# A two-layer graph kernel: h_prime turned by DMA, edge masks made on GpSimd, and layer 0 stretched over 42 steps

## The chip, the cores and the metric

The kernel runs on one core of one Trainium2 chip. The metric is the device time of one execution in microseconds (us), as the median of three runs. A core has five engines that run side by side and wait for each other with semaphores: TensorE (PE in the profile, with PEld for its weight loads), VectorE (DVE), ScalarE (ACT), GpSimd (POOL) and SyncE (SP), which here only issues DMAs. Sixteen DMA engines move data between the chip's main memory (HBM) and the on-chip memory (SBUF). TensorE writes its results to another on-chip memory, PSUM.

## The reference

There are 16 batches of 1024 nodes with 128 features each, and an adjacency matrix of zeros and ones per batch. Two layers follow each other. Everything is float32. Cut to what matters:

```python
# layer 0, B, N, D = 16, 1024, 128
h = einsum('bnf,df->bnd', x, Ww) + Wb
e = einsum('bjl,bkl->bjk', einsum('bjd,dl->bjl', h, A), h)
e = e + swapaxes(e, 1, 2)                       # symmetric scores
scores = where(adj > 0, e, 0.0)
attention = softmax(scores, axis=1) * adj
h_prime = relu(einsum('bij,bjk->bik', attention, h))
ic = sigmoid(h_prime @ wi_u + x @ wi_x)[..., None]
fc = sigmoid(h_prime @ wf_u + x @ wf_x)[..., None]
oc = sigmoid(h_prime @ wo_u + x @ wo_x)[..., None]
x = layernorm(x + oc * tanh(ic * h_prime + fc * x))

# layer 1, H = 4 heads
h = einsum('bnf,hfd->hbnd', X, conv_w) + conv_b[:, None, None, :]
scores = einsum('hbni,hij,hbmj->hbnm', h, attn_w, h)
Ah = tanh(A[None] * scores)
hh = relu(einsum('hbnm,hbmd->hbnd', Ah, h))
x = layernorm(x + relu(relu(mean(hh, axis=0)) + X))
```

## The kernel before

The rows of a batch are worked on in eight blocks of 128. The main loop runs layer 1 of batch b, in 32 steps (4 heads by 8 blocks), and puts pieces of layer 0 of batch b+1 between the steps. One step of layer 1:

```python
def layer1_step(b, hd, m):
    ...
    for q in range(NH):                                   # two halves of 512 columns
        ps = ps_sc.tile([P, 512], F32, tag="sc", ...)     # four PSUM banks turn by turn
        nc.tensor.matmul(ps, x1T[:, ts(m, P)], uT[:, ts(q, 512)], start=True, stop=True)
        nc.vector.tensor_mul(s[:, ts(q, 512)], ps, adj[:, ts(q, 512)])
    nc.scalar.activation(s, s, AF.Tanh)
    def back(halves=range(NH)):
        for q in halves:
            nc.tensor.matmul(acc[:, ts(q, 512)], h1[:, ts(hd, D)], s[:, ts(q, 512)], ...)
    ...
    push(...)          # back is issued two steps later
```

A float32 matmul shows in the profile as two records, called passes below. A step is thus eight passes of 512 columns.

The pieces of layer 0 have letters: L loads xT and the eight adjacency tiles of a batch, X loads x, Q and H project, S makes a block of scores (upper triangle), T turns it into the lower triangle, A masks and exponentiates a block, B multiplies it by the adjacency and feeds the matmul of the block before, R is the relu, P and p bring h_prime from columns to rows, G makes the gates, and I, O, V, N make the output and its layernorm.

```python
def mask(j):                                              # A
    s = t["R"][:, :, j, :]
    if ("edge", j) in t:                                  # batch 0
        ... nc.vector.tensor_tensor_reduce(s[:, ks], s[:, ks], t["edge", j][:, ks], 1.0, top, ALU.mult, ALU.max, highest)
        nc.vector.tensor_scalar_mul(nmax, highest, -1.0)
    else:                                                 # all other batches
        nc.vector.scalar_tensor_tensor(s, adj, 0.0, s, op0=ALU.is_gt, op1=ALU.mult)
        nc.vector.tensor_reduce(nmax, s, AX.XY, ALU.max, negate=True)
    nc.scalar.activation(s, s, AF.Exp, bias=nmax, accum_out=t["z", j])

def weigh(j):                                             # B
    nc.vector.tensor_mul(s, s, adj_t[b][j]...)            # line 353
    nc.vector.reciprocal(rz, t["z", j])
    nc.scalar.mul(t["hz", j], t["h"][:, j, :D], rz)
    if j:
        back(j - 1)                                       # four passes of 512 columns

def rows_hp(groups):                                      # P, p: h_prime to rows, by TensorE
    for ks in groups:
        for i, k in enumerate(ks):                        # ident_g: identity and the three w*_u columns
            nc.tensor.matmul(pt[:, i, :], t["hpT"][:, ts(k, P)], ident_g, start=True, stop=True)
        nc.scalar.copy(t["hp"][:, ks[0] : ks[-1] + 1, :], pt)
```

In batch 0 the edges (adjacency above zero, as bf16) are made by GpSimd in `find_edges`, one `tensor_scalar` per block. Other turns go without TensorE: VectorE transposes within 32x32 squares, one DMA writes the result to HBM, and four DMAs read it back in the other order.

```python
def turn(dst, src, name):
    t = sb.tile([P, N], F32, tag="turn", bufs=2, ...)
    nc.vector.transpose(t..., src)
    nc.sync.dma_start(d, t)
    for c in range(P // Q):                               # 4
        nc.sync.dma_start(dst[ts(c, Q)]..., dv[c])
```

The plan of the steps, and the loop:

```python
BETWEEN = [
    "H0 H1 H2", "S0", "T0 S1", "T1 S2", "T2 A0", "S3 B0", "T3 A1", "S4 B1",
    "T4 A2", "S5 B2", "T5 A3", "S6 B3", "T6 A4", "S7 B4", "A5", "B5",
    "A6", "B6", "A7", "B7", "X R", "P", "p G", "I0",
    "O0", "V0", "N0", "", "", "", "", "",
]
AHEAD = {28: "L", 31: "Q0 Q1"}                            # for batch b+2
TURN = 27                                                 # x1 of batch b+1 is turned
ENDING = (DELAY, DELAY + 3, DELAY + 5, DELAY + 7)         # end of layer 1 of batch b-1
for b in range(B):
    after = layer0(b + 2) if b + 2 < B else {}
    for step in range(H * NB):
        hd, m = divmod(step, NB)
        layer1_step(b, hd, m)
        ...                                               # rows(b, second half) in step 0
        run(nxt, BETWEEN[step])
        if step == TURN and b + 1 < B: turn_x1(b + 1)
        run(after, AHEAD.get(step, ""))
        ...                                               # head_uT once a head, rows(b+1, first half) in step 31
```

Ahead of the loop stands a start in which layer 0 of batch 0 runs alone and that of batch 1 begins.

Of the kernel before, what the change touches and what calls it, by code (L numbers as in the profile page):

```python
# [11 lines left out]
F32 = mybir.dt.float32  # L12
BF16 = mybir.dt.bfloat16
AF = mybir.ActivationFunctionType
# [4 lines left out]
P = 128  # L19
# [4 lines left out]
def two_layer_adjacency_kernel(  # L24
# [44 lines left out]
    a_in = consts.tile([P, P], F32, name="a_in")  # L69
    nc.sync.dma_start(a_in, A)  # L70
    ww_in = consts.tile([P, P], F32, name="ww_in")
# [19 lines left out]

    def load_late_weights():
        nc.sync.dma_start(cw_in[0:1], conv_b.rearrange("(o h) d -> o h d", o=1))
        nc.sync.dma_start(cw_in[1:P], conv_w[:, 0 : D - 1, :].rearrange("h f d -> f h d"))
        nc.sync.dma_start(cw_last, conv_w[:, D - 1 : D, :].rearrange("h f d -> f h d"))
        nc.sync.dma_start(aw, attn_w.rearrange("h i j -> i h j"))

# [6 lines left out]
    but_first = consts.tile([1, P], F32, name="but_first")  # L104
# [10 lines left out]
    a_sym = consts.tile([P, P], F32, name="a_sym")  # L115
    s_ww = consts.tile([P, P], F32, name="s_ww")
# [3 lines left out]
    b_wide = consts.tile([P, P], F32, name="b_wide")  # L120
# [116 lines left out]
    def layer0(b):  # L237
# [7 lines left out]
        def load():  # L245
            t["xT"] = sb.tile([P, N], F32, tag="xT", name=f"xT_{b}")
            nc.sync.dma_start(t["xT"], xT[b])
            adj_t[b] = []
            for j in range(NB):
                a = adjp.tile([P, N], F32, tag="adj", name=f"adj_{b}_{j}")  # L250
                nc.sync.dma_start(a, adjT[b, ts(j, P), :])
                adj_t[b].append(a)
# [72 lines left out]
        def find_edges(j):  # L325

            m = sb.tile([P, N], BF16, tag="h1", name=f"edge_{b}_{j}", bufs=NB + 1)
            nc.gpsimd.tensor_scalar(m, adj_t[b][j], 0.0, None, ALU.is_gt)
            t["edge", j] = m.rearrange("p (k d) -> p k d", d=P)

        def mask(j):
            s = t["R"][:, :, j, :]
            nmax = sb.tile([P, 1], F32, tag="nmax", name=f"nmax_{b}_{j}", bufs=4)
            if ("edge", j) in t:
                top = -3e38
                for q, ks in enumerate((ts(0, BH), ts(1, BH)) if j == 0 else [slice(NB)]):
                    highest = sb.tile([P, 1], F32, tag="highest", name=f"highest_{b}_{j}_{q}", bufs=4)
                    nc.vector.tensor_tensor_reduce(
                        s[:, ks], s[:, ks], t["edge", j][:, ks], 1.0, top, ALU.mult, ALU.max, highest
                    )  # L340
                    top = highest
                nc.vector.tensor_scalar_mul(nmax, highest, -1.0)
            else:
                adj = adj_t[b][j].rearrange("p (k d) -> p k d", d=P)
                nc.vector.scalar_tensor_tensor(s, adj, 0.0, s, op0=ALU.is_gt, op1=ALU.mult)  # L345
                nc.vector.tensor_reduce(nmax, s, AX.XY, ALU.max, negate=True)  # L346
            t["z", j] = sb.tile([P, 1], F32, tag="z", name=f"z_{b}_{j}", bufs=4)
            nc.scalar.activation(s, s, AF.Exp, bias=nmax, accum_out=t["z", j])  # L348

        def weigh(j):  # L350

            s = t["R"][:, :, j, :]
            nc.vector.tensor_mul(s, s, adj_t[b][j].rearrange("p (k d) -> p k d", d=P))  # L353
            rz = sb.tile([P, 1], F32, tag="rz", name=f"rz_{b}_{j}", bufs=4)
            nc.vector.reciprocal(rz, t["z", j])  # L355
            t["hz", j] = sb.tile([P, D], F32, tag="hz", name=f"hz_{b}_{j}", bufs=4)
            nc.scalar.mul(t["hz", j], t["h"][:, j, :D], rz)  # L357
            if j:
                back(j - 1)
# [27 lines left out]
        def gates():  # L387

            gate = t["gate"]
            gflat = gate.rearrange("p k g -> p (k g)")  # L390
            nc.vector.tensor_add(gate, t["hp"][:, :, D : D + 3], gate)
            nc.scalar.activation(gflat, gflat, AF.Exp, scale=-1.0)
            nc.vector.tensor_scalar_add(gflat, gflat, 1.0)
            nc.vector.reciprocal(gflat, gflat)  # L394
            t["u"] = sb.tile([P, NB, D], F32, tag="u", name=f"u0_{b}", bufs=1)
            t["x1"] = sb.tile([P, NB, D + 1], F32, tag="x1", name=f"x1_{b}")
            for ks in PARTS:
                nc.gpsimd.tensor_mul(  # L398
                    t["u"][:, ks], t["x"][:, ks],
                    gate[:, ks, 1:2].to_broadcast([P, ks.stop - ks.start, D]),  # L400
                )
            nc.gpsimd.memset(t["x1"][:, :, 0:1], 1.0)

# [21 lines left out]
        def finish(p):  # L425
# [7 lines left out]
            "L": load, "X": load_x, "R": relu,  # L433
            "P": lambda: rows_hp(GROUPS[:-1]), "p": lambda: rows_hp(GROUPS[-1:]),
            "G": gates,
        }
        for i, ks in enumerate(GROUPS):
            pieces[f"H{i}"] = partial(project_h, [ks])
# [7 lines left out]
        for j in range(NB):  # L446
            for name, piece in (("S", score), ("A", mask), ("B", weigh)):
                pieces[f"{name}{j}"] = partial(piece, j)
            if b == 0:
                pieces[f"E{j}"] = partial(find_edges, j)  # L450
            if j + 1 < NB:
                pieces[f"T{j}"] = partial(turn_score, j)
# [40 lines left out]
    def layer1_step(b, hd, m):  # L493
        x1T, h1, uT = x1T_t[b], h1_t[b, m], u_t[b, hd]
        adj = adj_t[b][m]
# [62 lines left out]
    def last_end(b, k0, k1):  # L558
# [19 lines left out]
    run(first, "L X")  # L578
    load_late_weights()
    run(second, "L")  # L580
# [8 lines left out]
    run(first, "P p G")  # L589
# [14 lines left out]
    run(second, "T0 T1 T2")  # L604
# [4 lines left out]
    BETWEEN = [  # L609
        "H0 H1 H2", "S0", "T0 S1", "T1 S2", "T2 A0", "S3 B0", "T3 A1", "S4 B1",  # L610
        "T4 A2", "S5 B2", "T5 A3", "S6 B3", "T6 A4", "S7 B4", "A5", "B5",
        "A6", "B6", "A7", "B7", "X R", "P", "p G", "I0",
        "O0", "V0", "N0", "", "", "", "", "",
    ]
    AHEAD = {28: "L", 31: "Q0 Q1"}
    TURN = 27
    ENDING = (DELAY, DELAY + 3, DELAY + 5, DELAY + 7)
    end, nxt = None, second
    for b in range(B):
        after = layer0(b + 2) if b + 2 < B else {}  # L620
        for step in range(H * NB):
            hd, m = divmod(step, NB)
            layer1_step(b, hd, m)
            if b and step == 0:
                rows(b, range(NB // 2, NB))
            if end is not None and step in ENDING:
                next(end, None)
            run(nxt, BETWEEN[step])
            if step == TURN and b + 1 < B:
                turn_x1(b + 1)  # L630
            run(after, AHEAD.get(step, ""))
            if hd == H - 1 and b + 1 < B:
                if m == NB - 1:
                    head_uT(b + 1, 0)
                    rows(b + 1, range(NB // 2))
            elif hd < H - 1 and m == NB - 4:
                head_uT(b, hd + 1)
# [55 lines left out]
```

## Time and profile before

| What | Value |
|---|---|
| time, median of three runs | 2448.36 us (2446.39 to 2449.8) |
| span of the profiled execution | 2444.8 us |
| granted TensorE clock, mean | 0.999 of full |
| mean DMA rate | 74 GB/s |
| DMA packets | 409,057, of which 352,630 are under 512 B |

"Busy" is the time in which an engine has at least one instruction under way. A line of the groups gives source line, engine, operation, operands and count, then busy time and the mean duration of one. The costliest groups on VectorE, ScalarE and GpSimd that the change touches are these.

| Line | Engine | What | Count | Mean ns |
|---|---|---|---|---|
| L345 | DVE | mask, batches 1 to 15 | 120 | 1195 |
| L346 | DVE | maximum, batches 1 to 15 | 120 | 1220 |
| L338 | DVE | fused mask and maximum, batch 0, whole blocks | 7 | 1210 |
| L353 | DVE | weighing by adjacency | 128 | 1240 |
| L328 | POOL | edges, batch 0 | 8 | 2950 |
| L384 | PE | h_prime to rows, passes of 131 columns | 256 | 275 |
| L385 | ACT | copy of these rows, two sizes | 32 and 16 | 488 and 378 |
| L398 | POOL | x times forget gate, batches 1 to 15 | 15 | 1900 |
| L556 | POOL | issue of an output store | 15 | 970 |

Durations of matmuls overlap, since the next begins before the last has drained. How long a matmul holds TensorE is read from the starts.

### The profile page before, as it was taken

To read this page: it belongs to the slowest core of one execution; us is meant where nothing else is said; L and a number is where in the kernel's file an instruction comes from. 1 tells how busy PE (TensorE), PEld (TensorE's weight loads), DVE (VectorE), ACT (ScalarE), POOL (GpSimd) and SP (SyncE) were. 2 spreads that over 40 slices of the span, in tenths; PEclk is the share of its full clock that TensorE was granted. 3 is DMA by queue.
4 is the path that set the end of the run, shared out by engine and by line. 5 is a ranking of instruction groups with operands and counts; after the bars stand their busy time and mean duration, and the time that the engine had idled before them with its cause. 6 is when DMAs were issued, how large, how long until landed. Compare 5 with 4: busy or idle time off the path is not lost.

```text
span 2444.8 us, 19911 instructions
## 1 busy us (share of the span) xinstructions
PE 2427.2 (99%) x6175; PEld 1121.6 (46%) x6175; DVE 1585.3 (65%) x3026; ACT 1083.9 (44%) x1522; POOL 136.5 (6%) x102
## 2 busy tenths in 40 slices
PE   8999999999999999999999999999999999999998
PEld 4444444444444444444444444444444444444444
DVE  6665847657586565866658666585765857658454
ACT  6444444344444444434444444444444444444432
POOL 4000000000000000000000000000000000000000
PEclk9999999999999999999999999999999999999999
DMA  4204124051230512304133140332404223042000
GB/s 174 60 10 145 45 95 95 1 151 39 95 95 9 148 34 101 89 21 142 27 108 81 52 124 15 119 70 72 106 12 128 62 95 84 11 135 55 17 26 9
DMA packets 409057, 180.77 MB, mean 74 GB/s; under 512 B 352630, under 2 KB 377078, under 8 KB 408951
## 3 DMA queue, kind: packets, MB, share of 16 engines
q1 hardware_dynamic: 405927, 171.63, 25.2%
q0 software_dynamic: 2160, 7.87, 0.8%
q8 instruction: 49, 0.80, 0.1%
q14 instruction: 57, 0.47, 0.1%
q10 hardware_dynamic: 864, 0.00, 0.0%
HBM read 127.80 MB, written 51.64 MB: 73 GB/s over the span
## 4 chain that ended last, share of the span: by engine, by line
PE 94%; DVE 2%; DMA 2%; SPq 1%; issue 0%; POOL 0%; ACT 0%; POOLq 0%; DVEq 0%
PE sc L510 34%; PE acc L516 34%; PE acc L365 9%; PE sc L288 5%; PE pT_u L201 4%; PE pR L481 4%; PE pT_q L201 1%; PE pt L384 1%; PE pR_h L272 1%; DMA xT<-in_xT_dram 1%; SPq L230 1%; DMA dram_x<-turn_x 0%; DVE st L184 0%; DVE x L192 0%; POOL rs L189 0%
## 5 line engine op out<-in xcount | busy, mean ns | idle before, releaser
L511 DVE TENSOR_TENSOR s<-sc,adj 128x512 f32<-128x512 f32 x1008 | 671.5, 685 | 623.0 <-PE sc L510 611.0
L510 PE MATMUL sc<-uT,x1T 128*128 128x512 f32 x2048 | 962.0, 592 | 0.0
L516 PE MATMUL acc<-s,h 128*128 128x512 f32 x2016 | 947.3, 592 | 0.0
L512 ACT ACTIVATE s<-s 128x1024 f32<-128x1024 f32 x504 | 533.0, 1057 | 806.9 <-DVE s L511 800.5
L516 PEld LDWEIGHTS acc<-s,h 128*128 128x128 f32 x2016 | 381.7, 190 | 483.5 <-issue 474.4
L510 PEld LDWEIGHTS sc<-uT,x1T 128*128 128x128 f32 x2048 | 385.7, 190 | 468.8 <-issue 421.7
L365 PE MATMUL acc<-R,hz 128*128 128x512 f32 x512 | 241.1, 593 | 1.5 <-ACT hz L357 1.4
L348 ACT ACTIVATE R<-R,nmax 128x1024 f32<-128x1024 f32 x128 | 147.0, 1149 | 201.9 <-DVE nmax L346 182.2
L353 DVE TENSOR_TENSOR R<-R,adj 128x1024 f32<-128x1024 f32 x128 | 158.7, 1240 | 5.7 <-issue 0.3
L346 DVE TENSOR_REDUCE nmax<-R 128x1 f32<-128x1024 f32 x120 | 146.4, 1220 | 4.1
L288 PE MATMUL sc<-xT,qT 128*128 128x512 f32 (+3 forms) x384 | 146.5, 491 | 0.5 <-ACT R L291 0.5
L365 PEld LDWEIGHTS acc<-R,hz 128*128 128x128 f32 x512 | 95.6, 190 | 108.0 <-issue 85.1
L345 DVE SCALAR_TENSOR_TENSOR R<-adj,R 128x1024 f32<-128x1024 f32 x120 | 143.3, 1195 | 0.0
L189 POOL TENSOR_TENSOR rs<-rs,mhalf 128x8 f32<-128x8 f32 (+2 forms) x35 | 65.8, 1881 | 1207.0 <-DVE rs L188 948.3
L291 ACT ACTIVATE R<-sc,h 128x512 f32<-128x512 f32 (+1 forms) x192 | 109.4, 579 | 39.2 <-PE sc L288 37.7
L201 PE MATMUL pT_u<-x1T,ms 128*128 128x512 f32 x256 | 120.4, 592 | 0.0
L481 PE MATMUL pR<-cw,x1T 128*128 128x512 f32 x256 | 114.9, 592 | 0.0
L357 ACT ACTIVATE hz<-h,rz 128x128 f32<-128x128 f32 x128 | 51.3, 400 | 128.7 <-DVE rz L355 128.4
L288 PEld LDWEIGHTS sc<-xT,qT 128*128 128x128 f32 x384 | 70.1, 192 | 70.4 <-issue 58.0
L484 ACT COPY h<-pR 128x512 f32<-128x512 f32 x128 | 75.0, 586 | 41.7 <-PE pR L481 41.7
L398 POOL TENSOR_TENSOR u<-x,gate 128x1024 f32<-128x1024 f32 (+1 forms) x17 | 30.6, 1799 | 969.4 <-DVE gate L394 969.4
L534 DVE SCALAR_TENSOR_TENSOR sum<-acc,sum 128x512 f32<-128x512 f32 x95 | 61.2, 686 | 33.8 <-PE acc L516 32.9
(109 smaller groups left out, 1035.2 us busy)
## 6 DMA issues: line engine op xcount, KB each, us to landing
adj<-in_adjT_dram SPq DMA_DIRECT2D x128, 512.0 KB, 7.7
xT<-in_xT_dram SPq DMA_DIRECT2D x16, 512.0 KB, 4.5
x<-in_x_dram SPq DMA_DIRECT2D x16, 512.0 KB, 4.2
dram_x<-turn_x SPq DMA_DIRECT2D x15, 512.0 KB, 2.6
x1T<-dram_x SPq DMA_DIRECT2D x60, 128.0 KB, 3.1
dram_sum<-turn_sum SPq DMA_DIRECT2D x15, 512.0 KB, 2.6
y<-dram_sum SPq DMA_DIRECT2D x60, 128.0 KB, 3.1
out_dram<-y POOLq DMA_DIRECT2D x15, 512.0 KB, 3.5
```

Source lines behind the costliest of these rows:

```text
L201: nc.tensor.matmul(ps, w, src[:, ts(q, 512)], start=True, stop=True)
L288: nc.tensor.matmul(ps[:, : at - lo], t["qT"][:, ts(j, P)], t["xT"][:, lo:at], start=True, stop=True)
L345: nc.vector.scalar_tensor_tensor(s, adj, 0.0, s, op0=ALU.is_gt, op1=ALU.mult)
L346: nc.vector.tensor_reduce(nmax, s, AX.XY, ALU.max, negate=True)
L348: nc.scalar.activation(s, s, AF.Exp, bias=nmax, accum_out=t["z", j])
L353: nc.vector.tensor_mul(s, s, adj_t[b][j].rearrange("p (k d) -> p k d", d=P))
L365: nc.tensor.matmul(t["acc"][:, ts(q, 512)], t["hz", j], t["R"][:, ts(q, BH), j, :], start=(j == 0), stop=(j == NB - 1),)
L481: nc.tensor.matmul(ps, x1T_t[b][:, ts(k, P)], cw.rearrange("p h d -> p (h d)"), start=True, stop=True)
L510: nc.tensor.matmul(ps, x1T[:, ts(m, P)], uT[:, ts(q, 512)], start=True, stop=True)
L511: nc.vector.tensor_mul(s[:, ts(q, 512)], ps, adj[:, ts(q, 512)])
L512: nc.scalar.activation(s, s, AF.Tanh)
L516: nc.tensor.matmul(acc[:, ts(q, 512)], h1[:, ts(hd, D)], s[:, ts(q, 512)], start=(m == 0), stop=(m == NB - 1),)
```

## The change

The change has four parts and a few moves of buffers.

1. In batches 1 to 15 h_prime gets to rows by a turn and a hop through HBM (`turn_hp`), not by `rows_hp` on TensorE. The products with the three gate vectors, which `ident_g` used to give along with the rows, are made by GpSimd (a multiplication with a broadcast vector) and VectorE (a sum along features). It is meant to take work from TensorE.
2. In all batches GpSimd makes the edges, as bytes in batches 1 to 15, and VectorE masks and takes the maximum in one instruction.
3. Layer 0 of a batch is spread over 42 steps: it begins in step 17 of the loop two batches earlier (`AHEAD`) and goes on to step 26 of the next one. Batch 1, which starts later, has a denser plan of its own (`FIRST`). It is meant to give the longer path of h_prime its room.
4. The adjacency tiles are loaded one by one, from GpSimd's queue from batch 2 on, each two steps ahead of its edges.

The diff, cut to its core:

```diff
-        def load():
-            t["xT"] = ...; nc.sync.dma_start(t["xT"], xT[b])
-            for j in range(NB): ... nc.sync.dma_start(a, adjT[b, ts(j, P), :])
+        def load_xT(): ...
+        def load_adj(j):
+            a = adj_t[b, j] = adjp.tile([P, N], F32, tag="adj", name=f"adj_{b}_{j}")
+            (nc.sync if b < 2 else nc.gpsimd).dma_start(a, adjT[b, ts(j, P), :])
 ...
         def find_edges(j):
-            m = sb.tile([P, N], BF16, tag="h1", ...)
+            if b == 0: m = sb.tile([P, N], BF16, tag="h1", ...)
+            else:      m = sb.tile([P, N], U8, tag="edge", ...)      # two buffers
 ...
         def mask(j):
-            (batch 0 fused, others scalar_tensor_tensor and tensor_reduce)
+            s, nmax = t["R"][:, :, j, :], -3e38
+            for ks in (ts(0, BH), ts(1, BH)) if (b, j) == (0, 0) else [slice(NB)]:
+                nc.vector.tensor_tensor_reduce(s[:, ks], s[:, ks], t["edge", j][:, ks], 1.0, nmax, ALU.mult, ALU.max, top)
 ...
+        def turn_hp():
+            t["hp"] = sb.tile([P, NB, D], F32, tag="hp", ...)
+            turn(t["hp"]..., hpT, f"hp_{b}")
+        def weigh_hp():
+            for g in (1, 0, 2):
+                t["hw", g] = sb.tile([P, NB, D], F32, tag="turn", ..., bufs=2)
+                nc.gpsimd.tensor_mul(t["hw", g], t["hp"], wu_b[:, g : g + 1, :].to_broadcast([P, NB, D]))
+        def sum_hp(g):
+            nc.vector.tensor_reduce(hw, t["hw", g], AX.X, ALU.add)
+            nc.vector.tensor_add(gate, hw, gate)
+        def gate_f():   sum_hp(1); sigmoid(t["gate"][:, :, 1:2]); forget()
+        def gate_i():   sum_hp(0)
+        def gates_io(): sum_hp(2); sigmoid(t["gate"][:, :, 0:3:2])
 ...
+        if b == 0: pieces.update(P=lambda: rows_hp(GROUPS), G=gates)
+        else:      pieces.update(P=turn_hp, Y=weigh_hp, F=gate_f, i=gate_i, o=gates_io)
 ...
+        for g, w in enumerate((wi_u, wf_u, wo_u)):        # with the late weights, at the start
+            nc.sync.dma_start(wu_b[:, g, :], w.partition_broadcast(P))
 ...
-    BETWEEN = [...]; AHEAD = {28: "L", 31: "Q0 Q1"}
+    BETWEEN = {
+        0: "L7 E5 B1 A3 T5 S6", 1: "B2", 2: "E6 A4", 3: "B3 S7 T6", 4: "E7 A5", 5: "B4", 7: "A6",
+        8: "B5", 10: "A7 B6", 11: "B7", 12: "X R", 13: "P", 16: "Y", 18: "F", 19: "i", 20: "o",
+        21: "I0", 22: "O0", 23: "V0", 26: "N0",
+    }
+    AHEAD = {
+        17: "W", 18: "Q0 Q1", 19: "H0 H1 H2", 20: "S0", 21: "T0 S1", 22: "S2", 23: "S3", 24: "T1",
+        25: "L0 T2 S4", 26: "L1", 27: "L2 E0 T3", 28: "L3 E1 S5", 29: "L4 A0 E2 T4",
+        30: "L5 A1 E3", 31: "L6 B0 A2 E4",
+    }
+    FIRST = {
+        0: "E1 A0 T3 S4", 1: "E2 B0 A1 T4 S5", 2: "E3 A2 T5 S6", 3: "E4 B1 A3 T6 S7",
+        4: "E5 B2 A4", 5: "E6 B3 A5", 6: "E7 B4 A6", 7: "B5 A7",
+    }
-    ENDING = (DELAY, DELAY + 3, DELAY + 5, DELAY + 7)
+    ENDING = (DELAY, 6, 12, 14)
+        plan = BETWEEN if b else {**BETWEEN, **FIRST}
```

Some tiles of the start that had buffers of their own (the weights `a_in`, `ww_in`, `a_sym`, `s_ww`, and `b_wide`, `but_first`) now share those of `hz` and `uT1`.

## Prediction

> **What bounds the kernel now.** I read the engine totals first. The columns are busy time, share of the span and instructions.
>
> ```profile
> span 2444.8 us, 19911 instructions
> PE 2427.2 (99%) x6175; PEld 1121.6 (46%) x6175; DVE 1585.3 (65%) x3026; ACT 1083.9 (44%) x1522; POOL 136.5 (6%) x102
> ```
>
> TensorE (PE) is busy 99% of the time and the next engine, VectorE (DVE), 65%. A busy TensorE can still be a slow one, because overlapping matmuls count as busy, so I went on to its waits (engine, line, releaser; total, times, longest).
>
> ```profile
> PE pw L122 <- DMA a_in<-in_L_gnn_A_dram: 3.2, 1, 3.2
> PE pt L565 <- DVE sum L534: 1.6, 1, 1.6
> PE pT_q L201 <- DMA xT<-in_xT_dram: 1.6, 5, 0.7
> PE acc L365 <- ACT hz L357: 1.4, 4, 0.5
> ```
>
> These are the four longest of eleven entries, and the eleven add up to 11 us. Only the third lies in the steady part of the program: TensorE reaches `pT_q` at the end of a batch slightly before the x tile has landed. The others are start and end.
>
> Then the timeline of TensorE near the end of layer 0 of one batch (start, busy time, what, how many).
>
> ```profile
> 761.40 1.88 PE L510 MATMUL sc<-uT,x1T 128*128 128x512 f32 x4
> 763.12 1.88 PE L516 MATMUL acc<-s,h 128*128 128x512 f32 x4
> 764.84 1.50 PE L384 MATMUL pt<-ident_g,hpT 128*128 128x131 f32 x12
> 766.18 1.88 PE L510 MATMUL sc<-uT,x1T 128*128 128x512 f32 x4
> 767.89 1.88 PE L516 MATMUL acc<-s,h 128*128 128x512 f32 x4
> 769.61 0.61 PE L384 MATMUL pt<-ident_g,hpT 128*128 128x131 f32 x4
> 770.06 1.88 PE L510 MATMUL sc<-uT,x1T 128*128 128x512 f32 x4
> ```
>
> Here starts matter, not durations. Four 128x512 passes occupy 763.12 - 761.40 = 1.72 us, so 0.43 us each, with or without layer 0 work between them. Twelve 128x131 passes take 766.18 - 764.84 = 1.34 us, which is 0.112 us each. Taking 381 columns off saves 0.318 us, or 0.833 ns a column, and 3 ns are left over per pass. So the pass rate is set by columns streamed and nothing waits.
>
> Last, busy time of each engine in two whole batches.
>
> ```profile
> 350.00:500.40 150.40, 150.40 (x381) 69.31 (x380) 99.34 (x188) 67.17 (x94) 7.05 (x5) 1.00 0.27 77
> 500.40:650.80 150.40, 150.40 (x381) 69.23 (x380) 99.36 (x188) 67.26 (x95) 7.05 (x5) 1.00 0.28 77
> ```
>
> After the stretch come its length, then PE, PEld, DVE, ACT and POOL, clock, DMA share and GB/s. A batch costs 150.40 us. The passes of a batch in the code give the same: 32 steps x 8 passes, 16 for `head_uT`, 16 for `rows`, 4 for `project_q` and 32 for layer 0's `back` are 324 x 0.4295 = 139.2; the scores are 9216 columns in 24 passes, 7.75; `project_h` 16 x 0.1125 = 1.8; `rows_hp` 1.79. Sum 150.5. The kernel is TensorE's own work plus a start of about 70 us and a short end.
>
> **What the Trainium skill says.** "Perfetto Trace Analysis", Identifying the Most-Contended Engine, warns that matmul busy share is no measure of distance from the limit and asks for weight-load share or useful work instead. The trace shows why (46% for weight loads beside 99%), so I rely on start-to-start times. "TensorE: Matmul & The Clock Gate", Back-to-back issue gap, has a gap that is linear in columns with about 2.5 ns on top; the trace agrees on the form and the constant (3 ns), while the column costs 0.833 ns here, twice the page's, in each of an f32 matmul's two recorded passes. "SBUF — State Buffer", Who interferes with whom, says that VectorE with two SBUF inputs and a GpSimd instruction reading SBUF lock each other out. The start of the trace agrees only in part: while GpSimd makes edges without pause, the multiplication of line 353 takes 1.85 us instead of 1.22, less than a whole 2.8 us edge, and the fused mask keeps its 1.20 us. "DMA: Bandwidth & Descriptors", SWDGE vs HWDGE vs iDMA, says that GpSimd builds the descriptors of DMAs in its queue. The 15 output stores of the kernel before show it as 0.97 us of GpSimd each.
>
> **The change, part by part.**
>
> TensorE. In batches 1 to 15 `rows_hp` goes: 8 matmuls, 16 passes x 0.112 = 1.79 us a batch, x 15 = 26.9 us. Batch 0 keeps its own. `turn_hp`, as `turn_x1` does already, needs no TensorE. Nothing is added to it. This is the whole direct gain, since the other engines' savings lie beside a TensorE that doesn't wait. The x tile for `project_q` is now asked for in step 17 rather than after the turn of x1 at step 27, with DMA traffic low, so the 1.6 us of waits should go too.
>
> VectorE, per batch. Removed: 8 x (1.195 + 1.220) = 19.3 us of mask and maximum. Added: 8 x (1.21 + 0.08 + 0.15) = 11.5 for fused mask, accumulator read and negation, with durations from batch 0 of the same trace; one turn 1.23; three reductions 3 x 1.22 = 3.7; their small additions 0.5; a second sigmoid 0.5. That is 99.3 - 19.3 + 11.5 + 1.2 + 3.7 + 0.5 + 0.5 = 97.4. If all eight multiplications of line 353 meet an edge, 8 x 0.63 = 5 more. So 97 to 102 of 148.6 us: an even exchange, and not the bound.
>
> ScalarE loses three copies (2 x 0.488 + 0.378 = 1.35) and gains one small exponential, about 0.2. No matter.
>
> GpSimd, per batch: 7.05 now, plus eight edges of 2.76 to 3.2, plus three 128x1024 multiplications of 1.9, plus eight loads of 0.97: 43 to 46 us, or 30%. Edges and loads lie in steps 25 to 4, twelve steps. These last about 12 x 3.43 for layer 1, three `uT` (5.2), `rows` (6.9) and some 10 of layer 0, together about 63 us, against 8 x (3.0 + 0.97) = 32. It keeps up, if it isn't held.
>
> Slack of the new waits, a bare step being 8 x 0.4295 = 3.43 us. (a) h_prime: relu in step 12, turn in 13. The x1 turn in the trace writes at 790.50, reads from 793.18 to 795.92, and its last read takes about 3, so landing is 8 us after the issue, 9 with VectorE. Step 18, where VectorE first needs the product, is over 17 us after step 13; less 9 and 1.9 for GpSimd, 6 us are free. (b) Adjacency: load in step 25+j, edge in 27+j, so about 7 to 9 us against an estimated 1 + 4.2 (GpSimd's 0.97, and the 4.2 in which 512 KB of x landed). (c) Edge j to mask j is two steps, and with two edge buffers edge j+2 waits for mask j: 3 us of work in a whole step or more. (d) Batch 1, over eleven steps, has the shortest paths: four turns one after another on the sync queue, some 5.7 us each, for steps of 4 to 7 us. Here a few us may be lost, once.
>
> The sum: 2448.4 - 26.9 - 1.6, plus 1.5 allowed for the start (three broadcast weight loads now stand before batch 1's x in the queue) and for (d), gives 2421.4. A quick look at density: steps 21 to 27 ask VectorE for 3.3 to 4.9 us each while TensorE has 3.4 to 4.9 there, because the next batch's scores now fall in the same steps. That is close, but in the kernel before, VectorE was full for 20 us on end (690 to 710) without a TensorE wait.
>
> **The rivals.** First, VectorE held by GpSimd: if an edge comes late, the mask stands at the head of VectorE's queue, layer 1's multiplications queue behind it and TensorE runs out of its four score banks. For it: GpSimd's queue now holds loads that wait for tiles, edges that wait for loads and for masks. Against it: the two-step distances above. One wait of 2 us in each of 15 batches would more than cancel the gain (2451); 5 us would give 2496. Second, port contention stretches VectorE by 0.63 us in many more instructions than line 353, and the dense steps tip over: perhaps 0.5 to 1 us a batch, 2430 to 2437. Third, the hop is hidden but more small packets delay the other turns: the hop adds one turn to the nine of a batch (seven of scores, x1 and the sum), so perhaps a tenth to a DMA share of 0.27, which doesn't fill it; no change. Fourth, the smoother plan gains more than the passes removed: there is nothing to gain, as steady TensorE has only 1.6 us of waits.
>
> **Range and chances.** The floor is solid: 15 x 1.79 plus all 11 us of waits would be 2410, and a 2% gain needs 2399, so 0.02 for faster by over 2%. Upward, one small wait a batch gives 2430 to 2437, hence 2416 to 2434 for eight in ten. Slower than 2497 needs over 5 us a batch lost: 0.03.
>
> **What would show it.** Right: a batch period near 148.6 us, all of it TensorE busy; no `pt` matmuls beyond batch 0's 16 passes; the fused mask at about 1.2 us x120 more; GpSimd near 30%. Wrong: TensorE waits in every batch that go back to masks or edges, VectorE waits on GpSimd of over 2 us, line 353 at 1.85 or more throughout, or a start longer than 70 us by more than 2.

## The result, and the profile after

| | before | after |
|---|---|---|
| time, median | 2447.93 us (2446.39 to 2449.80, 4 runs) | 2502.64 us (2502.54 to 2503.06, 4 runs) |
| ratio after / before | | 1.0223, 95% interval 1.0206 to 1.0241 |
| span of the profiled execution | 2444.8 us | 2500.3 us |
| granted TensorE clock, mean | 0.999 | 0.987 |

The change made the kernel 2.2% slower. The prediction was 2421.4 us, so 81.2 us have to be found. The engine totals of the changed kernel (busy time, share of the span, instructions):

```profile
span 2500.3 us, 20182 instructions
PE 2428.7 (97%) x5935; PEld 1103.2 (44%) x5935; DVE 1606.2 (64%) x3266; ACT 1074.8 (43%) x1492; POOL 629.3 (25%) x379
```

TensorE has 240 passes fewer, which is 15 x 16 as planned, and yet more busy time. VectorE (64%) and GpSimd (25%) are no fuller than foreseen. The longest waits of TensorE in the changed kernel (what waits, line, what released it; total us, times, longest):

```profile
PE pT_u L207 <- DMA x1T<-dram_x: 45.0, 12, 4.5
PE pT_u L207 <- DVE nmax L349: 8.3, 2, 4.4
PE pw L128 <- DMA a_in<-in_L_gnn_A_dram: 3.2, 1, 3.2
```

The first two are new. `pT_u` is the first product of layer 1 of the next batch, `head_uT(b+1, 0)`, and its operand `x1T` is the turned x1. It waits once in 14 batches, 53.3 us in all. The second line is the same wait, at the same place and of the same length (3.9 and 4.4 us): in these two batches the record of a VectorE instruction happens to fall within 0.03 us of TensorE's start. TensorE's timeline at one such place (start, busy time, what, how many, and in brackets the wait ahead of it):

```profile
673.58 1.88 PE L557 MATMUL acc<-s,h 128*128 128x512 f32 x4
679.02 3.37 PE L207 MATMUL pT_u<-x1T,ms 128*128 128x512 f32 x4 [3.56 <-DMA x1T<-dram_x]
682.23 3.60 PE L522 MATMUL pR<-cw,x1T 128*128 128x512 f32 x8
```

TensorE stands for 3.56 us, and then the four passes of `pT_u` occupy 682.23 - 679.02 = 3.21 us instead of 1.72. That is a second loss, and the windows of the changed kernel show what goes with it. The columns are stretch, length, PE, PEld, DVE, ACT, POOL, granted clock, DMA share and GB/s. The first stretch runs from the issue of x1's write to that of its first read, the second from there to the start of `pT_u`, and the third holds `pT_u`'s passes.

```profile
666.50:672.70 6.20, 6.20 (x15) 2.66 (x14) 2.30 (x5) 2.66 (x4) 3.32 (x2) 1.00 0.75 204
672.70:679.00 6.30, 2.76 (x7) 0.96 (x6) 6.21 (x11) 3.76 (x5) 3.25 (x2) 0.96 0.93 206
679.00:682.20 3.20, 3.18 (x4) 1.44 (x5) 0.54 (x3) 1.83 (x3) 2.79 (x2) 0.55 0.66 188
```

After the wait the granted clock is 0.55. The records of the clock in this trace have it at half for 3.41 us at ten of the 14 waits and for twice that at the other four. Over the whole run the `pT_u` passes are busy 143.8 us against 120.4 before, and the `pR` passes 119.6 against 114.9: 28.1 us more. Waits 53.3 and slow passes 28.1 make 81.4, against a distance to the prediction of 81.2.

Why x1 is late is seen in the queue of SyncE. In the kernel before (start, time to issue, what, how many):

```profile
790.50 0.34 SPq L227 DMA_DIRECT2D dram_x<-turn_x  x1
793.18 2.74 SPq L230 DMA_DIRECT2D x1T<-dram_x  x4
795.97 0.82 SPq L247 DMA_DIRECT2D xT<-in_xT_dram  x1
796.83 4.73 SPq L251 DMA_DIRECT2D adj<-in_adjT_dram  x8
```

The loads of the next batch stand behind the hop of x1 in the same queue, so the write has no load beside it: 2.7 us until the reads are issued. In the changed kernel:

```profile
657.75 0.59 SPq L323 DMA_DIRECT2D dram<-turn  x1
663.27 2.82 SPq L326 DMA_DIRECT2D R<-dram  x4
666.50 0.32 SPq L233 DMA_DIRECT2D dram_x<-turn_x  x1
672.68 3.67 SPq L236 DMA_DIRECT2D x1T<-dram_x  x4
676.45 0.75 SPq L323 DMA_DIRECT2D dram<-turn  x1
```

A turn of scores (T2, first two lines) now goes ahead of x1: VectorE began to turn x1 at 662.09, but its write comes 4.4 us after that, when T2's reads have been issued. Then it takes 6.2 us. An adjacency load went out of GpSimd's queue at 665.82, 0.7 us ahead of the write. The median times from issue to landing in the changed kernel (KB each, us) say the same of all batches:

```profile
adj<-in_adjT_dram POOLq DMA_DIRECT2D x112, 512.0 KB, 4.4
...
dram_hp<-turn_hp SPq DMA_DIRECT2D x15, 512.0 KB, 2.6
...
dram_x<-turn_x SPq DMA_DIRECT2D x15, 512.0 KB, 6.3
x1T<-dram_x SPq DMA_DIRECT2D x60, 128.0 KB, 3.7
```

The write of h_prime has the size and form of x1's and lies in steps without loads: 2.6 us. x1's takes 6.3, where in the kernel before it took

```profile
dram_x<-turn_x SPq DMA_DIRECT2D x15, 512.0 KB, 2.6
```

One thing more lies on this path. The layernorm's last piece (`x<-u,mv,rs`), which the turn follows, has grown, as VectorE's groups show (busy us, mean ns of one | idle before). Before:

```profile
L192 DVE TENSOR_SCALAR x<-u,mv,rs 128x128 f32<-128x128 f32 x128 | 34.3, 341 | 10.0 <-POOL rs L189 9.8
```

After:

```profile
L198 DVE TENSOR_SCALAR x<-u,mv,rs 128x128 f32<-128x128 f32 x128 | 66.5, 726 | 0.1
```

In the batch above, its eight instructions take 4.39 us instead of 2.14, from 656.58, while GpSimd makes an edge (2.80 us from 657.51).

So the theory: x1's hop lost its slack to three things, (i) the layernorm stretched by an edge, (ii) a turn of scores ahead of it in the sync queue, (iii) adjacency loads beside its write and reads. The rivals: GpSimd's edges hold VectorE (the prediction's first rival); the removal of one cause is enough; or the third and fourth part of the change are at fault as a whole, and nothing in it gains.

### The profile page after: what moved, and what is told of

Read it like the earlier page. It is cut to its first block, busy times and chain, and to the rows that moved or that the text cites. A ratio compares the mean times of both kernels' runs of the same rounds, so it can differ in the third digit from the quotient of the medians.

```text
span 2500.3 us, 20182 instructions
## 1 busy us (share of the span) xinstructions
PE 2428.7 (97%) x5935; PEld 1103.2 (44%) x5935; DVE 1606.2 (64%) x3266; ACT 1074.8 (43%) x1492; POOL 629.3 (25%) x379
## 4 chain that ended last, share of the span: by engine, by line
PE 88%; DMA 7%; SPq 3%; DVE 1%; issue 0%; ACT 0%; POOL 0%; POOLq 0%; DVEq 0%; ACTq 0%
PE sc L551 32%; PE acc L557 31%; PE acc L368 8%; PE pT_u L207 5%; PE pR L522 5%; PE sc L294 4%; DMA dram_x<-turn_x 3%; DMA x1T<-dram_x 2%; SPq L236 1%; DMA dram<-turn 1%; PE pT_q L207 1%; PE pR_h L278 1%; SPq L99 1%; SPq L326 1%; DVE s L552 0%
## 5 line engine op out<-in xcount | busy, mean ns | idle before, releaser
L552 DVE TENSOR_TENSOR s<-sc,adj 128x512 f32<-128x512 f32 x1008 | 680.4, 686 | 702.7 <-PE sc L551 691.2
L337 POOL TENSOR_SCALAR edge<-adj 128x1024 uint8<-128x1024 f32 (+1 forms) x128 | 356.3, 2785 | 463.3 <-DVE top_None L344 455.3
L195 POOL TENSOR_TENSOR rs<-rs,mhalf 128x8 f32<-128x8 f32 (+2 forms) x35 | 54.6, 1561 | 973.7 <-DVE rs L194 973.7
L207 PE MATMUL pT_u<-x1T,ms 128*128 128x512 f32 x256 | 143.8, 691 | 53.4 <-DMA x1T<-dram_x 45.0
L344 DVE CUSTOM_DVE_ANT_0 R<-R,edge 128x1024 f32<-128x1024 f32 (+1 forms) x128 | 154.1, 1204 | 3.5 <-PE turn L312 3.4
L399 POOL TENSOR_TENSOR hw<-hp,wu_b 128x1024 f32<-128x1024 f32 x45 | 107.1, 2396 | 145.0 <-DVE s L552 44.6
L522 PE MATMUL pR<-cw,x1T 128*128 128x512 f32 x256 | 119.6, 612 | 0.0
L319 DVE STREAM_TRANSPOSE turn<-R 128x896 f32<-128x896 f32 (+6 forms) x105 | 73.6, 701 | 62.0 <-DMA dram_x<-turn_x 54.1
L207 PEld LDWEIGHTS pT_u<-x1T,ms 128*128 128x128 f32 x256 | 53.9, 218 | 126.3 <-issue 54.3
L258 POOL DMA_DIRECT2D adj<-in_adjT_dram x112 | 65.8, 588 | 133.6 <-DVE s L552 133.4
```

The lines of the kernel that those rows point to most:

```text
L207: nc.tensor.matmul(ps, w, src[:, ts(q, 512)], start=True, stop=True)
L337: nc.gpsimd.tensor_scalar(m, adj_t[b, j], 0.0, None, ALU.is_gt)
L522: nc.tensor.matmul(ps, x1T_t[b][:, ts(k, P)], cw.rearrange("p h d -> p (h d)"), start=True, stop=True)
```

## The experiments

Every kernel is the changed one with the edit shown. Those run several times have an interval against the kernel before on the same chip. The others ran once, which suffices for differences of 20 us and more: the widest of the repeated sets (the first experiment, 8 runs) spans 15 us.

**Start x1 earlier.** The layernorm goes from step 26 to 24, the turn of x1 from 27 to 25.

```diff
-        21: "I0", 22: "O0", 23: "V0", 26: "N0",
+        21: "I0", 22: "O0", 23: "V0", 24: "N0",
-    TURN = 27
+    TURN = 25
```

> Edit: the layernorm's last piece N0 moves from step 26 to 24 and the turn of x1 from step 27 to 25, nothing else. Theory (the turn of x1 lands too late for the first projection of the next batch, and that wait is the whole loss): the turn starts two steps (7 us) earlier, the wait was 3 to 4.5 us, so the wait and the slow clock behind it go; batch period 148.6 us, time 2419 to 2427. Rival (GpSimd's edges and waits hold VectorE, and TensorE waits for that): VectorE's steps 24 and 25 become denser, so the time stays at 2500 or gets worse.

Measured: 2454.75 us (2450.93 to 2466.11, 8 runs), ratio 1.0040 (1.0024 to 1.0056). 48 us came back and the wait at `pT_u` is gone. But the time isn't near 2421, since waits have moved. From the waits of this kernel (its profiled execution took 2464.67 us, 10 more than the median, so they are on the high side):

```profile
DVE turn L319 <- DMA dram<-turn: 50.9, 17, 4.5
...
PE pR L522 <- ACT uT L209: 28.2, 14, 2.9
DVE turn L319 <- DMA dram_x<-turn_x: 24.7, 12, 5.0
```

VectorE stands 75.6 us before turning scores, because both buffers for turned tiles are held by writes that haven't landed. ScalarE's copy of `uT` then comes late, and TensorE waits for it one step behind `pT_u`. That the buffers cause it is the reading here; the three-buffer version below tests it.

**No adjacency traffic.** From batch 2 on a batch uses the tiles of the batch two before it. It leaves out 112 of the 128 adjacency loads, and all later batches are computed with the adjacencies of the first two, so only its time is of use.

```diff
         def load_adj(j):
+            if b >= 2:
+                adj_t[b, j] = adj_t[b - 2, j]
+                return
```

> Edit: the adjacency loads of batches 2 to 15 are left out; these batches use the tiles of batch b-2, so the output is of other adjacencies, and the DMA engines carry 59 MB less. Theory (the loads share the DMA engines with the turn of x1 and stretch it): the write of x1 lands in 2.6 to 3.3 us, not 6.2, the score turn before it in the queue is 2 us shorter too, together more than the wait of 3 to 4.5 us; time 2420 to 2430. If the order of the sync queue or the stretched layernorm on VectorE is enough to make the wait, 2450 to 2500.

Measured: 2423.79 us, x1's write 2.9 us in the mean. All of the loss is gone. But the edges no longer wait for loads and moved too (the layernorm is back at 2.13 us), so (i) and (iii) are taken away together. A later run separates them.

**x1 ahead of the turns of scores.**

```diff
-        25: "L0 T2 S4", 26: "L1", 27: "L2 E0 T3", 28: "L3 E1 S5", 29: "L4 A0 E2 T4",
-        30: "L5 A1 E3", 31: "L6 B0 A2 E4",
+        25: "L0 S4", 26: "L1", 27: "L2 E0", 28: "L3 E1 T2 S5", 29: "L4 A0 E2 T3",
+        30: "L5 A1 E3 T4", 31: "L6 B0 A2 E4",
```

> Edit: the score turns T2, T3, T4 of the batch after next move from steps 25, 27, 29 to 28, 29, 30, behind the turn of x1 in the sync queue. Theory (in the queue x1 stands 3 us behind the reads of T2): the write of x1 is issued about 3 us earlier, but still takes some 6 us beside the loads; wait 0.5 to 1.5 us a batch, time 2430 to 2450. If the order in the queue doesn't matter, 2500.

Measured: 2482.51 us, 20 us less than the changed kernel, and a miss. x1 is now nearly in time (0.1 us of wait a batch at `pT_u`). But the three turns have been crowded behind x1's write, which still takes 5.0 us beside loads, and VectorE waits for their buffers. TensorE loses 31.8 us at `pR` to ScalarE's copy of `uT` and 6.7 more to VectorE. The layernorm is as stretched as before (725 ns a piece). The queue's order alone is not the cure.

**No edges on GpSimd.** Batches 1 to 15 mask as the kernel before did.

```diff
         def find_edges(j):
+            if b: return
 ...
+                nc.vector.scalar_tensor_tensor(s, adj, 0.0, s, op0=ALU.is_gt, op1=ALU.mult)
+                nc.vector.tensor_reduce(nmax, s, AX.XY, ALU.max, negate=True)
```

> Edit: batches 1 to 15 make no edges on GpSimd and mask with two VectorE instructions as the kernel before did (8 us more of VectorE a batch); the loads stay on GpSimd's queue. Theory: the last piece of the layernorm takes 2.1 us again instead of 4.4, but x1 still stands behind T2 in the sync queue and beside the loads, so the wait stays within 1 us of what it was: 2490 to 2505. Rival (edges on GpSimd hold VectorE or take its port): without them the time falls to 2420 to 2430.

Measured: 2527.40 us, 25 us slower than the changed kernel and outside both ranges: late edges are not what costs the time. TensorE waits at `pT_u` for 50.1 + 19.7 us. The layernorm is short again, and x1's turn starts 2 us earlier, but its write is issued 6.3 us after the turn instead of 4.4, since T2's hop ahead of it now takes longer: the loads are no longer spaced by edges. That last step is argued from the times of issue.

**A third buffer for turned tiles.** (The tile xT moves to one buffer to make room, and that of batch 1 into one of x1T's.)

```diff
-    tag="turn", bufs=2
+    tag="turn", bufs=3                 # all tiles of this tag
-            t["xT"] = sb.tile([P, N], F32, tag="xT", ..., bufs=2)
+            t["xT"] = sb.tile([P, N], F32, tag=("x1T" if b == 1 else "xT"), ...)
```

> Edit: the changed kernel with three buffers for the turns, not two (room for the third comes from xT, which needs one buffer after the start). There are two ways from slow writes to TensorE's wait: x1 itself lands late, or VectorE stands at a score turn until a buffer is free (62 us in all in the changed kernel) and layer 1 waits behind it. If the first carries the loss, the third buffer takes VectorE's waits away but x1 stands where it stood in the queue: 2480 to 2503. If the second carries it: 2421 to 2440.

Measured: 2538.45 us, a miss in the other direction. VectorE's waits for buffers are gone, and TensorE's wait grew to 81.6 us. With slow passes, (146.6 - 120.4) + (124.3 - 114.9) = 35.6 us, that makes 117 us, the distance to the prediction. Turn, write issue and write of x1 are as in the changed kernel (table below); it is the reads that take 2.2 us longer (8.8 against 6.6). In the changed kernel a load is issued at 678.48, 5.8 us after the first read; here at 682.86, 1.5 us after it. VectorE's wait for a buffer had held back masks, hence edges, hence loads. The link from wait to loads is argued from issue times, not shown by a run.

**Both: x1 early and three buffers.**

> Edit: x1 two steps earlier (as in the first experiment) and three buffers for the turns. With x1 early, 28 us of TensorE's waits were left, at the copy of uT on ScalarE, behind VectorE, which stood 75 us at score turns for a buffer. If that is the second way, it goes with the third buffer: 2420 to 2430. If what is left comes from late masks or edges, 2445 to 2455.

Measured: 2423.07 us (2422.06 to 2423.70, 4 runs), ratio 0.9904 (0.9889 to 0.9918). It joins the first edit and the fifth, each of which alone is slower than the kernel before. No steady TensorE wait is left, and a batch, from the windows of this kernel, is

```profile
641.00:789.90 148.90, 148.90 (x365) 67.39 (x365) 97.47 (x205) 66.19 (x92) 40.01 (x24) 1.00 0.36 85
```

148.90 us with TensorE busy in all of it, as the prediction had it (148.6). With this plan the third buffer removes what the first edit left, as the first experiment's reading has it.

**x1 early, two buffers, later loads.** The last four loads and their edges go to later steps.

```diff
-        0: "L7 E5 B1 A3 T5 S6", 1: "B2", 2: "E6 A4", 3: "B3 S7 T6", 4: "E7 A5", ...
+        0: "L5 E4 B1 A3 T5 S6", 1: "B2", 2: "L6 E5 A4", 3: "B3 S7 T6", 4: "L7 E6 A5", ..., 6: "E7",
-        ... 29: "L4 A0 E2 T4", 30: "L5 A1 E3", 31: "L6 B0 A2 E4",
+        ... 29: "A0 E2 T4", 30: "L4 A1 E3", 31: "B0 A2",
```

> Edit: x1 two steps earlier, two buffers, and the last four adjacency loads later (steps 30, 0, 2, 4, not 29 to 0) with their edges later too, still two steps before each mask. Theory (loads and turns share the DMA engines): fewer loads lie beside the turns T2 to T4, their writes land sooner, VectorE waits under 30 us for buffers; time 2422 to 2440. If how many loads lie there doesn't matter: 2450 to 2460.

Measured: 2429.24 us (2425.26 to 2431.06, 4 runs), ratio 0.9924 (0.9907 to 0.9940). Loads spread out do most of what the third buffer does: VectorE's waits for buffers fall from 75.6 to 40.2 us (under 30 were expected), TensorE's at `pR` from 28.2 to 4.8.

**All loads on the sync queue,** at the same steps.

```diff
-            (nc.sync if b < 2 else nc.gpsimd).dma_start(a, adjT[b, ts(j, P), :])
+            nc.sync.dma_start(a, adjT[b, ts(j, P), :])
```

> Edit: the changed kernel with all adjacency loads on the sync queue, at the same steps. Theory (it is the traffic, not the queue it is issued from): the writes of the turns stay at 5 us and more, and the turns stand behind the loads in one queue: 2490 to 2530. Rival (loads issued by GpSimd take precedence on the DMA engines or hold GpSimd): 2425 to 2450.

Measured: 2526.37 us. The time is in the range expected, but its cause is another than the theory had. From the waits of this kernel:

```profile
DVE R L344 <- POOL edge L337: 68.5, 19, 5.4
PE pR L522 <- ACT uT L209: 62.4, 14, 5.2
```

The loads stand behind turns in the queue, edges come late, and VectorE waits for GpSimd: the prediction's first rival, which appears in no other kernel but for one wait of 3.4 us at the start of the fourth experiment's. At these steps the loads are better off in GpSimd's queue.

**What the parts are worth in a plan without the wait.** Three variants of the kernel with x1 early and three buffers. First, part one of the change undone:

```diff
-        if b == 0: pieces.update(P=lambda: rows_hp(GROUPS), G=gates)
-        else:      pieces.update(P=turn_hp, Y=weigh_hp, F=gate_f, i=gate_i, o=gates_io)
+        pieces.update(P=lambda: rows_hp(GROUPS), F=gates) if b else pieces.update(P=lambda: rows_hp(GROUPS), G=gates)
```

> Edit: the version with x1 early and three buffers (2423 us), but with h_prime brought to rows by TensorE in all batches again, so part one of the change undone where no wait hides it. Prediction's term: 16 passes x 0.112 us x 15 batches = 26.9 us more, 2450. If the hop cost elsewhere what it saved, the difference is under 15 us.

Measured: 2448.14 us (2447.81 to 2449.49, 12 runs), ratio 1.0009 (1.0000 to 1.0017). Each set against its own kernel before, that is +1.9 and -24.0 us: the removed passes are worth 25.8 us. The prediction's term was 26.9.

Second, part two undone (the edit of the fourth experiment):

> Edit: x1 early and three buffers, but masks in two VectorE instructions and no edges on GpSimd in batches 1 to 15, so part two of the change undone: 8 us more of VectorE a batch. Theory: VectorE isn't the bound and the fused mask lies off the path: 2421 to 2430. If the denser plan needs the fused mask, VectorE falls behind in steps 29 to 2 and TensorE waits 1 to 4 us a batch: 2440 to 2490.

Measured: 2450.12 us (2448.21 to 2452.27, 20 runs), ratio 1.0015 (1.0009 to 1.0022). The rival was right. VectorE is busy 1674.9 us instead of 1561.5, 7.6 us more a batch, and from the waits

```profile
PE pR L532 <- ACT uT L209: 24.2, 14, 1.9
```

TensorE loses what the removed passes had brought. In the timeline of this kernel ScalarE, just ahead of its copy of `uT`, stands 1.97 us (to 667.88) for the maximum of a two-instruction mask, so it is VectorE's extra work that comes late here. This dense plan doesn't work without the fused mask; what the mask would bring in the old plan, no run shows.

Third, with the later loads:

> Edit: x1 early, three buffers, and the last four loads later as well. TensorE has no steady waits left in the version without the later loads, so nothing is to be gained: 2420 to 2424. If the writes still cost something small, up to 3 us less than 2423.

Measured: 2421.74 us (2421.62 to 2422.05, 4 runs), ratio 0.9901 (0.9884 to 0.9917). It is the fastest of all versions. That it lies within 0.4 us of the 2421.4 predicted is in part luck, since on this chip the kernel before took 2446.28 and not 2448.4: the gain is 24.5 us, and 27.0 were predicted.

**Separating the causes.** Three runs on (i), (ii) and (iii). Only the layernorm moves, to step 25, ahead of the edges; x1's turn stays at 27:

```diff
-        21: "I0", 22: "O0", 23: "V0", 26: "N0",
+        21: "I0", 22: "O0", 23: "V0", 25: "N0",
```

> Edit: the changed kernel with the layernorm's last piece in step 25, not 26, so that no edge runs beside it; the turn of x1 stays in step 27. Theory: that piece takes 2.1 us, not 4.4, but x1 stands behind the reads of T2 in the sync queue anyway, so its write is issued at most 1 us earlier: 2485 to 2503. If the stretch of VectorE by the edge sets the start of the turn: 2.2 us earlier in each batch, 2455 to 2475.

Measured: 2459.18 us, 43 us less than the changed kernel. The layernorm's pieces take 347 ns in the mean (726 after), x1's turn starts 2.0 us earlier, and TensorE's wait falls from 53.3 to 27.2 us. The theory was wrong here (2485 to 2503) and the rival right, though the write of x1 is hardly faster (6.0 us against 6.3).

Loads without traffic: as the second experiment, but each left-out load is replaced by an instruction of GpSimd that sets one column of the tile to zero and has the load's waits. It too computes with the adjacencies of the first two batches, less that column.

```diff
         def load_adj(j):
+            if b >= 2:
+                a = adj_t[b, j] = adj_t[b - 2, j]
+                nc.gpsimd.memset(a[:, 0:1], 0.0)
+                return
```

> Edit: as the run without adjacency loads (batches 2 to 15 use the tiles of batch b-2, so other adjacencies), but each load is replaced by a one-column memset on GpSimd, which waits for the same VectorE instruction as the load did; it sets that column to zero. So the edges run when they ran in the changed kernel and the traffic is gone. If traffic and the edge beside the layernorm add up (the run with an early norm got back 43 us, the one without loads 79, but that one moved the edges too): the norm takes 4.4 us, the writes 3, and some wait is left: 2430 to 2460. If without the traffic the queue has room enough to take up the 2.2 us: 2421 to 2428.

Measured: 2422.22 us, as the second expectation had it, with no waits at `pT_u`. The sync queue keeps its order in the program and an edge still runs beside the layernorm, yet x1's write takes 2.8 us and is issued 1.3 us after the turn, because T2's hop ahead of it is short too. The layernorm is still stretched, though only to 3.00 us, since the edge now begins 0.4 us ahead of it and not 0.9 us behind. The other 1.4 us would not have mattered: the last of x1's reads lands 5.5 us after the first is issued, and TensorE needs it after 10.5. Without the traffic there is no loss.

Last, the layernorm at step 25 and T2 to T4 behind x1, with every load in place:

```diff
-        21: "I0", 22: "O0", 23: "V0", 26: "N0",
+        21: "I0", 22: "O0", 23: "V0", 25: "N0",
         (and T2, T3, T4 in steps 28, 29, 30, as in the third experiment)
```

> Edit: the changed kernel, all loads as they were, with the norm in step 25 (no edge beside it) and T2, T3, T4 behind the turn of x1 in the queue. Traffic alone is left. If start of the turn and place in the queue are enough against it: x1 lands in time, and only VectorE's waits for a turn buffer are left, 2423 to 2445. If traffic alone makes x1 late: 2450 to 2482.

Measured: 2423.04 us, the lower end of the first range. With two buffers and all the traffic, the loss is gone. The sync queue of this kernel:

```profile
643.59 0.33 SPq L233 DMA_DIRECT2D dram_x<-turn_x  x1
646.25 5.63 SPq L236 DMA_DIRECT2D x1T<-dram_x  x4
```

The write takes 2.66 us although a load goes out of GpSimd's queue 0.24 us after it. So traffic isn't sufficient either: what counts is what the write stands behind. Layernorm alone gives 43 us, order alone 20, both 80. By the times of issue the two help each other: with the earlier start the write goes out 3.05 us after one load and just ahead of the next, and with the later start (third experiment) 0.88 us behind one.

Means over the turns of x1 of batches 1 to 14 (at that of batch 15 no loads are left), in us, from the timelines; "due" is when TensorE would have started `pT_u` had it not waited:

| kernel | turn starts before due | turn to write issue | write to first read | first read to start of `pT_u` | wait |
|---|---|---|---|---|---|
| before | 13.7 | 1.3 | 2.8 | 9.6 | 0 |
| after | 13.4 | 4.4 | 6.3 | 6.5 | 3.8 |
| order (third) | 13.2 | 1.3 | 5.0 | 7.0 | 0.1 |
| no edges (fourth) | 15.5 | 6.3 | 6.4 | 7.8 | 5.0 |
| three buffers (fifth) | 13.4 | 4.2 | 6.2 | 8.8 | 5.8 |
| layernorm at 25 | 15.4 | 4.0 | 6.0 | 7.4 | 1.9 |
| no traffic, one column set | 14.6 | 1.3 | 2.8 | 10.5 | 0 |
| layernorm at 25, and order | 15.3 | 1.3 | 2.8 | 11.2 | 0 |
| x1 early, three buffers | 20.7 | 3.0 | 4.3 | 13.4 | 0 |

Where nothing waited, the fourth number contains the slack.

In the twelve kernels whose loads go out of GpSimd's queue (the changed one and eleven of the edits), each write of x1 is set here against the last load issued ahead of it, and against the four reads of a score turn ahead of it in the sync queue (12 x 14 writes, from write to first read):

| last load ahead of the write | last of a turn's reads ahead | writes | lowest, median, highest |
|---|---|---|---|
| under 2 us | 2 us or more | 18 | 4.8, 5.0, 5.9 us |
| under 2 us | under 2 us | 56 | 4.6, 6.2, 7.5 us |
| 3 us or more | 3 us or more (all in the last kernel, "layernorm at 25, and order") | 14 | 2.6, 2.7, 3.7 us |
| 3 us or more | under 2 us | 78 | 3.5, 3.9, 7.2 us (63 of them up to 4.4) |

Two writes lie between. A load takes about 4.4 us itself, so a write behind one that is 3 us old meets only its end. A turn's reads ahead of the write cost it something too, but only beside loads: in the kernels without loads, writes 0.7 to 2.0 us behind such reads took 2.6 to 3.3 us. Why 15 of the 78 took over 5 us stays open: age of the load and reads ahead are the same for the quick ones. Nor was the arbitration between the two queues tried by itself.

## Why the prediction was wrong

**TensorE's term held.** 26.9 us predicted, 25.8 measured. The start (about 70 us predicted; the main loop's first product comes at 70.5 in the trace) and the period without waits (148.6 against 148.9) held too, and so did the x tile asked for earlier: its waits fell from 1.6 to 0.9 us.

**VectorE's term held, GpSimd's was too high.** 97 to 102 us a batch were predicted for VectorE and 97.5 measured in the plan without waits; 43 to 46 for GpSimd against 40.0. On GpSimd the load's issue costs 0.59 us rather than 0.97, and the multiplications 2.40 rather than 1.90.

**The failed step is "Slack of the new waits".** It lists waits that the change adds, (a) to (d), and none of these cost anything in the steady part. The wait that cost 53.3 us is an old one: TensorE for the turned x1. The change gave it no instruction and no new step, but new neighbours in its queue, on the DMA engines and beside the layernorm that it follows. The kernel before had 9.6 us from the first read to the need, of which the reads took 5.8 (until the last had landed, mean of the eight batches whose records have it): 3.8 us of slack. Against that stand 0.3 us of a later start, 3.1 more ahead of the write's issue, 3.5 more for the write, and 0.7 for the reads (6.5 against 5.8): 7.6 - 3.8 = 3.8, the wait of 3.8 us a batch. The sum has to come out, since these intervals make up the whole path; what the trace tells is the share of each, and the write and what stands ahead of it are most of it. The stretched layernorm does not show as a term, because the new plan would have started the turn earlier than the old one: at 15.4 us with the layernorm out of the way.

**The third rival named the right thing and was dismissed by an average.** It said that the hop adds "perhaps a tenth to a DMA share of 0.27, which doesn't fill it; no change". In the steps of x1's hop the share is 0.75 to 0.93, and what counts there is a single write and what was issued just ahead of it. The prediction took its 8 us to landing from x1's hop in the kernel before, where no load ran beside the write. For the new hop of h_prime, in steps without loads, that held (2.6 us for the write); for x1's own, in the new plan, it was not asked again.

**The second rival had the right kind and the wrong place.** It looked for a longer multiplication at the weighing by adjacency. That takes 1.236 us in the mean after the change, against 1.240. It is the layernorm's `tensor_scalar` that grew, by 385 ns x 8 = 3.1 us of summed durations and (66.5 - 34.3) / 15 = 2.1 us of busy time a batch. The prediction cited only the sentence of the Trainium skill, "SBUF — State Buffer", Who interferes with whom, on two SBUF inputs. The same list names `tensor_scalar`, with one input, among those that can take the port pair shared with GpSimd, where their operands allow a two-port mode. The trace agrees that it is hit, though not that it is held for a whole edge of 2.80 us: eight pieces grew by 2.25 us together, and the longest single one in the run took 1.57 us. That the port is the reason is the page's account; the runs show only that the pieces are slow beside an edge. What these 2 us were worth was mis-sized as well, at "0.5 to 1 us a batch": they lie on x1's path, and the run that moves them out of the way gains 43 us, 2.9 a batch.

**A wait costs more than itself.** "One wait of 2 us in each of 15 batches" was put at 30 us. Here 53.3 us of waits brought 28.1 of slow passes with them, half as much again. The prediction had no term for that.

**The first rival didn't happen.** In the changed kernel VectorE never waits for an edge: of the 3.6 us of idle time ahead of the fused mask in all batches, 3.4 go back to TensorE at the start.

## What to carry to other kernels

When a change moves transfers, look at every old transfer on the way to the bound engine that shares a queue or a step with them, and count its slack from issue to need with the durations it will have beside the new traffic, not those it had alone. Busy shares, averaged over a batch, tell nothing of that. A change that slowed the kernel may need no undoing: moving one instruction group by a step and three turns behind x1 turned +2.2% into -0.9% (one run, 2423.04 us against 2444.77 for the kernel before).

## What the hardware showed that I had not expected

- A 512 KB write to HBM takes 2.6 to 3.7 us alone or, in one plan, just ahead of a load, and 4.6 to 7.5 us (74 writes) when issued under 2 us behind a 512 KB load, though the two come from different queues. The Trainium skill, "DMA: Bandwidth & Descriptors", Issuing engines are not separate DMA queues, says that DMAs run on the same 16 engines and interleave, whichever engine started them; these durations agree with that.
- Taking away a wait of VectorE (the third buffer alone) made the kernel 36 us slower; by the times of issue, the wait had kept a load off the critical reads. With x1 early the same buffer gained 32 us.
- A TensorE wait can bring a half clock behind it, and does not always. In the changed kernel it followed all 14 waits (3.05 to 4.46 us) and cost 28.1 / 14 = 2.0 us each. After shorter waits it came or stayed away: with the layernorm at 25, five of twelve waits were followed by it, one of 1.96 us among them, and one of 2.76 us was not. The twelve passes after the waits of 2.76 and 1.96 us, in the windows of the kernel with the layernorm at 25 (clock third from the end):

```profile
517.40:522.62 5.22, 5.21 (x12) 2.36 (x13) 0.00 (x0) 3.74 (x7) 2.76 (x2) 1.00 0.82 187
668.21:675.13 6.92, 6.92 (x13) 2.95 (x13) 0.00 (x0) 3.77 (x7) 2.80 (x2) 0.75 0.80 194
```

One stretch of 3.41 us at half clock costs 6.92 - 5.22 = 1.70 us here. What decides is not the length of the wait alone. In every trace here with more than one such stretch they start whole multiples of 3.41 us apart, so they lie on a fixed grid (in the changed kernel the first four start at 214.3, 367.9, 524.9 and 678.5 us, which is 45, 46 and 45 cells apart). Take the cells between 100 and 2400 us, in all traces, that are at full clock and in which TensorE stands idle for 0.3 us or more. In all 74 with 1.88 us of idle time or more the next cell is at half clock, in none of the 105 with 1.83 us or less. The wait of 1.96 us lies within one cell, that of 2.76 us in two, with 1.82 us in the larger part.
